# Four edits in the last two thirds of a graph-network kernel: chunk ends two products later, new PSUM places, spread stores, mixed rows inside a pass

## The chip, the core and the metric

The kernel runs on one NeuronCore of a Trainium2 chip. TensorE (PE) multiplies, VectorE (DVE) and ScalarE (ACT) work elementwise, GpSimd (POOL) and SyncE (SP) mostly start DMAs. Everything is float32. The metric is the device time of one execution in microseconds; the number compared is the median of the runs.

## The reference

N = 2708 nodes with 128 features, and a weighted sparse adjacency matrix `adj` (2708 x 2708) that is held dense. Four residual layers:

```python
x = layernorm(x + L0(x, adj))   # Laplacian product, 4 nearest neighbours, Laplacian product with them
x = layernorm(x + L1(x, adj))   # attention
x = layernorm(x + L2(x, adj))   # normalised Laplacian product
x = layernorm(x + L3(x, adj))   # relu([x, adj @ x] @ W.T + b)

# L1:
XW = X @ W
Z1 = leaky_relu((XW @ a[f:])[:, None] + (XW @ a[:f])[None, :], 0.01)
den = exp(Z1);  num = A @ den
att = where(num != 0, den / num, 0)
H = A @ (att @ XW)
```

## The kernel before

**Layout.** `adj` lies transposed in DRAM (`adjT`). A product with `adj` runs over 22 row tiles of 128 rows (the last, `FULL`, has 20 rows) and over six column chunks (four of 512 columns, one of 384, one of 276). `res` keeps the last six row tiles in SBUF, the others stream through the four slots of `ring`, one panel of four row tiles at a time, loaded by SP (L178). The 20 rows of the last tile are spread over three groups of partitions (`few`), so that the last-tile products of three chunks stand together.

**`by_panels` (L189)** is the pass that is run for the last three products with `adj`. For each chunk `c` it makes one product per row tile (L204; a float32 product is two matrix instructions) into a PSUM tile of the pool `acc`. In chunks 0 and 3 the last-tile products of three chunks follow (i == FULL). When a chunk is complete it calls `done(c, acc)`, which is `into_hT` (L231): ACT copies the chunk to `hT`/`gb` (L234), then `then(c, tiles)` runs: `end_layer1` transposes (L1794), `end_layer2` and `end_layer3` multiply by a weight (L285), and DVE, POOL and ACT do the norm. The passes are not in a hand-written order: the Tile scheduler places the instructions, so chunks 1, 2, 4 and 5 have the first product of the next chunk between their copy and what reads it; chunks 0 and 3 have nothing there.

**The attention loop (`block_layer`).** Ranking makes the matrix of L1 sparse enough for blocks: 44 steps (two column halves `h` of 22 steps `q`), in an order written out by hand for all engines. In step i, `load(i + 2)` fetches two gathers of rows by POOL (L1133) and, by SP, two short rows each from the table `carry` (L1140); POOL fetches rows of XW (L1113); PE finds `num` (L1699) for the narrow piece of step i and the wide piece of step i+1, then adds step i-1 into `hacc` (L1581); ACT inverts `num` with Ln and Exp (L1556, L1559); DVE corrects and weighs (L1566, L1570, L1573); SP stores two rows of each result back into `carry` (L1714). The narrow `num` has one PSUM buffer, the wide one two, `hacc` three banks. All of them come from one pool `ops`, so the wide buffers lie in banks 0 to 3, the narrow in bank 4, `hacc` in 5 to 7.

**The loop's head.** Before the loop, `add_line` (L1430) sums the whole matrix into two PSUM banks; `end_half(1)` copies the second to SBUF by ACT (L1450, L1451), SP sends it to `carry` in four DMAs (`send_half`, L1459) and loads last rows of `adjT` back into `res` (L1549), of which the scheduler leaves three on SP after the sends. Then every engine reads `flag` (L1592) and branches (L1851) into the arm that holds the loop. The first steps of the loop are the fill of a pipeline.

**Between the loop and the passes.** ACT and DVE copy `hacc` to `mT` (L160, L162), PE transposes twelve tiles of it (L1782), DVE scales them into `mixed`, which is the same place as `carry` (L1783). The first ten tiles were mixed already in the loop's last step (L1765, L1767). Then `by_panels(rows_of(mixed), ...)` begins. `acc2` (three banks) and `mis2` (five) are the pools of the passes.

## Time and profile before

| what | us |
|---|---|
| median of 3 runs | 1047.29 (1046.78 to 1047.69) |
| the profiled execution, its time | 1047.87 |
| its span, from first to last instruction | 1046.1 |
| PE busy | 980.2 (94%) |
| DVE, ACT, POOL busy | 638.9, 332.6, 263.4 |
| mean granted TensorE clock | 0.977 |
| up to the loop's head | 0 to 488 |
| attention loop | 488 to 711 |
| three passes | 711 to 1046 |

PE's busy time includes time in which one instruction drains while the next streams. Idle PE time is what matters where the chain of work runs through PE. In a row of the timeline, the bracket at the end gives how long the engine was idle before, and what the profile takes for the releaser. A row with a count merges instructions that follow each other, so gaps can lie within it. "issue" means that nothing in the profile shows the wait.

### The profile page before, as it was taken

Reading aid. Unit: us, or ns where it says so; the run is one execution under the profiler, and the core shown is the slowest. Engines: PE = TensorE matmul, PEld = TensorE weight load, DVE = VectorE, ACT = ScalarE, POOL = GpSimd, SP = SyncE. Lnnn points to the kernel's source line nnn. Section 1 sums busy time; section 2 is a strip of 40 time slices with the busy share of each in tenths; the row PEclk is TensorE's granted clock in tenths of the full one; section 3 lists DMA queues with packets and bytes.
Section 4 is the critical chain, followed back from the end, with each engine's and each line's share of the span. In section 5 each row is a group of like instructions: output and inputs, shape, how many; then the busy total and the mean of one; then the engine's idle time right before and its main releaser. Section 6 shows DMA issues by size and latency. Waiting matters only on the chain.

```text
span 1046.1 us, 11657 instructions
## 1 busy us (share of the span) xinstructions
PE 980.2 (94%) x3773; PEld 478.0 (46%) x3773; DVE 638.9 (61%) x1364; ACT 332.6 (32%) x609; POOL 263.4 (25%) x339
## 2 busy tenths in 40 slices
PE   0899999999987999798999999999999999999996
PEld 0346544444433456554333333334445544564444
DVE  5876549999834579864999999993212121222222
ACT  0000236555401235504677776661101100020000
POOL 5000000000665564027766444420111100000000
PEclk9899999999997999799999999999999999999998
DMA  9998220000383657696555455556564856474652
GB/s 344 351 366 259 91 81 1 1 0 1 94 276 93 220 166 239 232 414 190 156 170 148 137 147 158 142 178 235 168 229 150 308 187 223 141 262 164 215 174 71
DMA packets 100401, 187.85 MB, mean 180 GB/s; under 512 B 13958, under 2 KB 43278, under 8 KB 100330
## 3 DMA queue, kind: packets, MB, share of 16 engines
q1 hardware_dynamic: 82296, 149.19, 42.4%
q0 software_dynamic: 17728, 37.62, 12.5%
q8 instruction: 32, 0.52, 0.2%
q14 instruction: 39, 0.32, 0.1%
q10 hardware_dynamic: 306, 0.20, 0.1%
HBM read 211.66 MB, written 4.16 MB: 206 GB/s over the span
## 4 chain that ended last, share of the span: by engine, by line
PE 49%; DVE 1%; ACT 1%; issue 0%; DMA 0%; POOL 0%; POOLq 0%; DVEq 0%
PE acc L204 28%; PE hacc L1581 10%; PE num L1699 10%; PE mis L285 1%; PE mis L1828 0%; DVE inv L1570 0%; ACT gb L234 0%; DVE err L1566 0%; PE mis L1794 0%; DVE inv L1573 0%; PE mis L1824 0%; DMA ring<-carry 0%; POOL rstd L253 0%; PE mis L1782 0%; ACT m_rows L160 0%
## 5 line engine op out<-in xcount | busy, mean ns | idle before, releaser
L1133 POOL DMA_INDIRECT ring<-in_adjT,slot_i x88 | 94.4, 1073 | 95.5 <-PE num L1699 73.7
L1699 PE MATMUL num<-ring,lw 128*64 128x512 f32 (+1 forms) x528 | 112.4, 556 | 3.9 <-DVE err L1566 1.9
L1581 PE MATMUL hacc<-inv,xws 128*128 128x512 f32 (+1 forms) x264 | 111.7, 559 | 0.3 <-DVE inv L1573 0.3
L724 PE MATMUL acc<-zT,z 128*128 128x512 f32 (+2 forms) x252 | 102.2, 552 | 0.0
L1556 ACT ACTIVATE inv<-num,plain 128x1024 f32<-128x1024 f32 x88 | 80.6, 916 | 57.6 <-PE num L1699 40.1
L253 POOL TENSOR_TENSOR rstd<-rstd,minus_half 128x4 f32<-128x4 f32 (+1 forms) x18 | 17.3, 961 | 313.4 <-DVE rstd L252 313.4
L234 ACT COPY gb<-acc 128x512 f32<-128x512 f32 (+2 forms) x18 | 9.6, 536 | 251.0 <-PE acc L204 251.0
L725 ACT COPY key<-acc 128x512 f32<-128x512 f32 (+2 forms) x126 | 67.2, 536 | 54.9 <-PE acc L724 27.6
L204 PE MATMUL acc<-ring,y 128*128 128x512 f32 (+2 forms) x192 | 83.7, 566 | 0.5 <-issue 0.5
L769 POOL DMA_INDIRECT got<-y_rows,where x66 | 71.5, 1084 | 41.7 <-DVE near_sum L782 20.5
L1581 PEld LDWEIGHTS hacc<-inv,xws 128*128 128x128 f32 x264 | 46.5, 189 | 77.6 <-issue 53.2
L1566 DVE TENSOR_TENSOR err<-inv,num 128x1024 f32<-128x1024 f32 x88 | 74.7, 854 | 8.5 <-ACT inv L1559 7.3
L204 PE MATMUL acc<-ring,xs 128*128 128x512 f32 (+2 forms) x192 | 78.1, 550 | 0.0
L1573 DVE SCALAR_TENSOR_TENSOR inv<-gb,g_inv,inv 128x1024 f32<-128x1024 f32 x88 | 77.0, 914 | 0.1
L204 PE MATMUL acc<-ring,carry 128*128 128x512 f32 (+2 forms) x192 | 74.5, 542 | 0.0
L204 PE MATMUL acc<-ring,m_rows 128*128 128x512 f32 (+2 forms) x192 | 74.3, 542 | 0.0
L1570 DVE SCALAR_TENSOR_TENSOR inv<-err,inv 128x1024 f32<-128x1024 f32 x88 | 72.5, 862 | 0.1
L724 PEld LDWEIGHTS acc<-zT,z 128*128 128x128 f32 x252 | 45.8, 190 | 50.4 <-issue 45.0
L1559 ACT ACTIVATE inv<-inv 128x1024 f32<-128x1024 f32 x88 | 67.7, 769 | 2.8
L1699 PEld LDWEIGHTS num<-ring,lw 128*64 128x64 f32 x528 | 35.8, 137 | 62.3 <-issue 47.6
L728 DVE MAX8 near<-key 128x8 f32<-128x2708 f32 x21 | 62.3, 2966 | 2.7 <-ACT key L725 2.7
L593 POOL TENSOR_TENSOR slot_e<-near,sim 128x44 f32<-128x44 f32 (+2 forms) x3 | 0.7, 240 | 248.9 <-DVE near L590 248.8
(379 smaller groups left out, 1361.7 us busy)
## 6 DMA issues: line engine op xcount, KB each, us to landing
ring<-in_adjT SPq DMA_DIRECT2D x71, 1024.0 KB
ring<-in_adjT SPq DMA_DIRECT2D x20, 677.0 KB
ring<-in_adjT SPq DMA_DIRECT2D x17, 768.0 KB
part<-in_adjT SPq DMA_DIRECT2D x12, 1024.0 KB
ring<-in_adjT SPq DMA_DIRECT2D x17, 552.0 KB
more<-in_adjT SPq DMA_DIRECT2D x10, 677.0 KB
res<-in_adjT SPq DMA_DIRECT2D x4, 1280.0 KB
part<-in_adjT SPq DMA_DIRECT2D x3, 768.0 KB
```

The lines of the kernel that those rows point to most:

```text
L204: nc.tensor.matmul(accs[c][: lhsT.shape[-1], :w], lhsT=lhsT, rhs=src, start=start, stop=stop)
L724: nc.tensor.matmul(pks[c][:p, : cw[c]], lhsT=z2[:, :p], rhs=zT[:, cs], start=False, stop=True)
L725: nc.scalar.copy(key[:p, cs], pks[c][:p, : cw[c]])
L769: nc.gpsimd.indirect_dma_start(out=got[:p, :], out_offset=None, in_=y2_rows[:, :], in_offset=bass.IndirectOffsetOnAxis(ap=where[:p, t, k : ...
L1133: nc.gpsimd.indirect_dma_start(out=rows[i][:KC, n, :], out_offset=None, in_=adj_half[:, :], in_offset=bass.IndirectOffsetOnAxis(ap=slot_i[ ...
L1556: nc.scalar.activation(inv, num[:, :w], AF.Ln, scale=plain[:, 0:1], bias=plain[:, 1:2])
L1559: nc.scalar.activation(inv, inv, AF.Exp, scale=-1.0)
L1566: nc.vector.tensor_mul(err, inv, num[:, :w])
L1570: nc.vector.scalar_tensor_tensor(inv, err, 2.0, inv, op0=ALU.subtract, op1=ALU.mult)
L1573: nc.vector.scalar_tensor_tensor(inv, gb[:, col : col + w], g_inv[:, q : q + 1], inv, op0=ALU.max, op1=ALU.mult)
L1581: nc.tensor.matmul(haccs[:, o:e], lhsT=xws[:, q, :], rhs=inv[:, o:e], start=(q == 0), stop=(q == NQ - 1))
L1699: nc.tensor.matmul(num[n * (BJ + 2) : (n + 1) * (BJ + 2), o:e], lhsT=lw[:, 2 * q + n, :], rhs=rows[i][:, n, c0 + o : c0 + e], start=True, ...
```

## The change

1. In `by_panels`, `done` now only copies and returns the rest; for chunks 0 and 3 the rest is run when two further products have been issued. For the other chunks it is run at once, as before.
2. The copy of the second half of the heads is made by DVE instead of ACT. The loop's PSUM pool is split into four: `hacc` in banks 0 to 2, the narrow `num` in bank 3, odd wide ones in 4 and 5, even ones in 6 and 7. In the passes `mis2` comes first (banks 0 to 4), `acc2` after it (5 to 7).
3. The four sends of the second half and the loads of the last rows are taken from the loop's head and given to SP one at a time, in steps 4 to 7 and 8 to 13. Six loads of last rows are now in the arm, where before three of them had been placed earlier.
4. The first pass begins with eight products of row tiles mixed in the loop; then come the twelve transposes with two products between them.

In the built program the order on POOL is the same as before; on ACT only the copy is gone; on DVE only the copy is new and the mixing has another line; PE has the same instructions in the order that 1 and 4 say.

```diff
-    def by_panels(weights, done, tick=None, ready=(), first=None):
+    def by_panels(weights, done, tick=None, ready=(), first=None, between=(0, None)):
...
+        pending = Due()
         def product(c, i, src, w):
+            pending.tick()
...
-                    done(c, accs[c])
+                    rest = done(c, accs[c])
+                    if rest is not None:
+                        pending.at(pending.n + 3, rest)
...
                 product(c, i, src, w)
+                if c == 0 and i + 1 == between[0]:
+                    between[1]()
                 if i == FULL - 1 and c % GROUPS:
-                    done(c, accs[c])
+                    rest = done(c, accs[c])
+                    if rest is not None:
+                        rest()
...
             nc.scalar.copy(hT[:, cols[c]], acc[:, : cw[c]])
-            then(c, chunk_tiles[c])
+            return lambda: then(c, chunk_tiles[c])
...
-            nc.scalar.copy(tot[:, : edges[4] - edges[3]], banks[h][:, : edges[4] - edges[3]])
-            nc.scalar.copy(tot[:64, edges[4] - edges[3] :], banks[h][:64, edges[4] - edges[3] : span])
+            copy = nc.vector.tensor_copy if h else nc.scalar.copy
+            copy(tot[:, : edges[4] - edges[3]], banks[h][:, : edges[4] - edges[3]])
+            copy(tot[:64, edges[4] - edges[3] :], banks[h][:64, edges[4] - edges[3] : span])
...
-        send_half(1, heads[1], nc.sync)
-        for c in range(C):
-            nc.sync.dma_start(res[few(c), FULL - S, cols[c]], adjT[FULL * P :, cols[c]])
+        right = heads[1]
...
-            tc.tile_pool(name="ops", bufs=1, space=bass.MemoryType.PSUM) as ops,
+            tc.tile_pool(name="hops", bufs=1, space=bass.MemoryType.PSUM) as hops,
+            tc.tile_pool(name="nops", bufs=1, space=bass.MemoryType.PSUM) as nops,
+            tc.tile_pool(name="odd", bufs=1, space=bass.MemoryType.PSUM) as odd,
+            tc.tile_pool(name="even", bufs=1, space=bass.MemoryType.PSUM) as even,
...
+            def num_tile(n, w, name):
+                pool = nops if w == NARROW else (even, odd)[n % 2]
+                return pool.tile([P, w], F32, tag=f"num{w}", name=name)
...
+                    if 4 <= i < 8:
+                        send_half(1, right, nc.sync, (i - 4,))
+                    elif i - 8 in range(C):
+                        last_rows_back((i - 8,))
...
+        mis_pool = arm.enter_context(tc.tile_pool(name="mis2", bufs=5, space=bass.MemoryType.PSUM))
         acc_pool = arm.enter_context(tc.tile_pool(name="acc2", bufs=3, space=bass.MemoryType.PSUM))
-        mis_pool = arm.enter_context(tc.tile_pool(name="mis2", bufs=5, space=bass.MemoryType.PSUM))
...
-        by_panels(rows_of(mixed), into_hT(end_layer1))
+        by_panels(rows_of(mixed), into_hT(end_layer1), between=(first // 4 * 4, mix_rows))
```

`mix_rows` holds the loop over the twelve tiles (transpose, scale) that stood before the first pass, and `last_rows_back(chunks)` the loads of the last rows. `Due.at(n, f)` runs f at the n-th tick.

More of the change, by code (lines that the diff above doesn't have):

```diff
@@ L225, in by_panels @@
                 product(c, i, src, w)
+                if c == 0 and i + 1 == between[0]:
+                    between[1]()
                 if i == FULL - 1 and c % GROUPS:
-                    done(c, accs[c])
+                    rest = done(c, accs[c])
+                    if rest is not None:
+                        rest()
                 if tick is not None:
                     tick()
+        assert not pending.work
     def into_hT(then):
@@ L1449, in end_half, with send_half @@
             tot = heads[h]
-            nc.scalar.copy(tot[:, : edges[4] - edges[3]], banks[h][:, : edges[4] - edges[3]])
-            nc.scalar.copy(tot[:64, edges[4] - edges[3] :], banks[h][:64, edges[4] - edges[3] : span])
+            copy = nc.vector.tensor_copy if h else nc.scalar.copy
+            copy(tot[:, : edges[4] - edges[3]], banks[h][:, : edges[4] - edges[3]])
+            copy(tot[:64, edges[4] - edges[3] :], banks[h][:64, edges[4] - edges[3] : span])
             if h == 0:
                 send_half(h, tot, nc.scalar)
-        def send_half(h, tot, queue):
-            for g in range(4):
+        def send_half(h, tot, queue, groups=range(4)):
+            for g in groups:
                 w = edges[g + 1] - edges[g]
@@ L1592, with last_rows_back @@
     over = nc.values_load(flag[0:1, 0:1], min_val=0, max_val=N)
+    def last_rows_back(chunks):
+        for c in chunks:
+            nc.sync.dma_start(res[few(c), FULL - S, cols[c]], adjT[FULL * P :, cols[c]])
     def dense_layer():
@@ L1606, in dense_layer @@
             nc.sync.dma_start(y2g[:LAST, FULL, :], y2_rows[FULL * P :, :])
+            last_rows_back(range(C))
             load_x(range(T))
@@ L1690, in block_layer @@
             nums, invs, haccs = {}, {}, {}
-            pieces = {"wide": (0, WIDE, 2), "narrow": (WIDE, NARROW, 1)}
+            pieces = {"wide": (0, WIDE), "narrow": (WIDE, NARROW)}
+            def num_tile(n, w, name):
+                pool = nops if w == NARROW else (even, odd)[n % 2]
+                return pool.tile([P, w], F32, tag=f"num{w}", name=name)
             def find_num(i, piece):
-                q, (c0, w, bufs) = steps[i][1], pieces[piece]
-                num = nums[i, piece] = ops.tile([P, w], F32, tag=f"num{w}", name="num", bufs=bufs)
+                q, (c0, w) = steps[i][1], pieces[piece]
+                num = nums[i, piece] = num_tile(i, w, "num")
                 for o in range(0, w, CW):
@@ L1707, in keep @@
             def keep(i, piece, err):
-                (h, q), (c0, w, _) = steps[i], pieces[piece]
+                (h, q), (c0, w) = steps[i], pieces[piece]
                 for n in range(2):
@@ L1720, in add @@
                 if q == 0:
-                    haccs[h] = ops.tile([P, 3 * CW], F32, tag="hacc", name="hacc")
-                for piece, (c0, w, _) in pieces.items():
+                    haccs[h] = hops.tile([P, 3 * CW], F32, tag="hacc", name="hacc")
+                for piece, (c0, w) in pieces.items():
                     add_up(w, q, invs[i, piece], haccs[h][:, c0 : c0 + w])
@@ L1748, in block_layer @@
                         errs = {}
-                        for piece, (c0, w, _) in pieces.items():
+                        for piece, (c0, w) in pieces.items():
                             errs[piece] = mix_1(w, nums[i, piece], invs[i, piece], own)
@@ L1753, in block_layer @@
                             mix_2(invs[i, piece], errs[piece])
-                        for piece, (c0, w, _) in pieces.items():
+                        for piece, (c0, w) in pieces.items():
                             mix_3(w, q, invs[i, piece], h * HALF + c0)
                     else:
-                        for piece, (c0, w, _) in pieces.items():
+                        for piece, (c0, w) in pieces.items():
                             mix_2(invs[i, piece], mix_1(w, nums[i, piece], invs[i, piece], own))
                             mix_3(w, q, invs[i, piece], h * HALF + c0)
-                for t0 in range(0, EARLY, WIDE // P):
+                for n, t0 in enumerate(range(0, EARLY, WIDE // P)):
                     ts = range(t0, min(t0 + WIDE // P, EARLY))
-                    pt = ops.tile([P, WIDE], F32, tag=f"num{WIDE}", name="pt", bufs=2)
+                    pt = num_tile(len(steps) + n, WIDE, "pt")
                     for t in ts:
@@ L1774, in two_layers, with mix_rows @@
         nonlocal acc_pool, mis_pool, hT
+        mis_pool = arm.enter_context(tc.tile_pool(name="mis2", bufs=5, space=bass.MemoryType.PSUM))
         acc_pool = arm.enter_context(tc.tile_pool(name="acc2", bufs=3, space=bass.MemoryType.PSUM))
-        mis_pool = arm.enter_context(tc.tile_pool(name="mis2", bufs=5, space=bass.MemoryType.PSUM))
         hT = gb
-        for t in range(first, T):
-            p = pw[t]
-            pt = mis_tile()
-            nc.tensor.transpose(pt[:p, :D], mT[:, t * P : t * P + p], ident)
-            nc.vector.tensor_scalar_mul(mixed[:p, t, :], pt[:p, :D], f_out[:p, t : t + 1])
-        spread(mixed[:, FULL, :])
+        def mix_rows():
+            for t in range(first, T):
+                p = pw[t]
+                pt = mis_tile()
+                nc.tensor.transpose(pt[:p, :D], mT[:, t * P : t * P + p], ident)
+                nc.vector.tensor_scalar_mul(mixed[:p, t, :], pt[:p, :D], f_out[:p, t : t + 1])
+            spread(mixed[:, FULL, :])
         inv_sqrt_of(dinv, deg, DEG_EPS)
+        if not first:
+            mix_rows()
         y3 = m_rows
```

## The prediction

> **What bounds the kernel now.** I read the page first, then the chain of work that ended last, then the timeline at its breaks.
>
> ```profile
> PE 980.2 (94%) x3773; PEld 478.0 (46%) x3773; DVE 638.9 (61%) x1364; ACT 332.6 (32%) x609; POOL 263.4 (25%) x339
> ```
>
> PE is the bound, so in its span of 1046.1 us the change can only win where PE stands idle or slow on the path: at the head of the attention loop, between loop and first pass, and at chunk ends. The chain through the head, and the timeline of PE there:
>
> ```profile
> 494.35 2.07 DMA ring<-carry
> ...
> 500.79 2.47 PE hacc L1581 x6
> 503.26 2.42 PE num L1699 x12
> ```
>
> ```profile
> 488.31 4.30 PE L1699 MATMUL num<-ring,lw 128*64 128x512 f32 x20 [0.74 <-issue]
> 494.50 0.78 PE L1699 MATMUL num<-ring,lw 128*64 128x330 f32 x4 [1.88 <-DVE err L1566]
> 496.55 4.24 PE L1699 MATMUL num<-ring,lw 128*64 128x512 f32 x8 [1.28 <-DMA ring<-carry]
> ```
>
> Three waits (the third ends 0.13 after the short load's landing): 0.74, 1.88 and 1.28 us. The eight instructions of the third row take 4.24 us. From 500.79 on, a step is 2.47 + 2.42 = 4.89 us and PE never waits until the loop's end. What stood before these rows on SP and ACT, and on DVE beside them:
>
> ```profile
> 488.06 0.15 ACT L1451 COPY m_rows<-acc 64x1 f32<-64x1 f32 x1
> 488.24 3.63 SPq L1459 DMA_DIRECT2D carry<-m_rows  x4
> 491.91 1.26 SPq L1549 DMA_DIRECT2D res<-in_adjT  x3
> 494.35 1.42 SPq L1140 DMA_DIRECT2D ring<-carry  x2
> 495.90 1.75 DVE L1573 SCALAR_TENSOR_TENSOR inv<-gb,g_inv,inv 128x1024 f32<-128x1024 f32 x2
> ```
>
> SP gave out seven DMAs, the flag and the branch before step 2's two short loads. And the clock granted around the third wait (columns: stretch, length, busy time of PE, PEld, DVE, ACT, POOL, then PEclk, DMA share, GB/s):
>
> ```profile
> 493.00:496.50 3.50, 0.78 (x4) 0.20 (x4) 3.50 (x5) 3.44 (x6) 2.99 (x3) 1.00 0.43 108
> 496.50:500.70 4.20, 4.15 (x8) 1.17 (x8) 4.20 (x7) 0.72 (x2) 3.28 (x4) 0.59 0.59 152
> ```
>
> Last, the chain from the loop's end into pass 1 and over the first chunk's end:
>
> ```profile
> 708.51 2.55 PE hacc L1581 x6
> ...
> 712.92 0.76 PE mis L1782 x5
> 713.69 0.86 PE acc L204 x2
> ...
> 716.17 17.46 PE acc L204 x44
> 733.63 0.59 ACT gb L234
> ```
>
> PE stands from 711.06 to 712.92 for three copies one after another, and again at 733.63 for one copy. A product (two instructions) is 0.86 us here.
>
> **The change part by part.**
>
> *Head, start of PE.* In the built program the first `num` waited for ACT's copy L1451, whose PSUM bank it reuses; that copy ended at 488.21 and PE's weight load began at 488.28. In the changed program it waits only for the loads of step 0, and the narrow and the odd piece for readers that ended by 486.3. What is left between the last matrix instruction (487.57) and the first one is flag and branch. No PE row shows their cost, so I bound it: nothing gives a gain of 0.74, all of it gives 0. DVE went through the same pair in 0.45 (487.41 after 486.96), ACT in 0.15; that is 0.29 and 0.59. I take 0.45, between these two nearest rows. DVE gets the copy (two instructions, 0.59 on ACT); it had nothing to do until 492.81 except one 0.18 us row for `dinv`, which then ends near 489, before POOL comes to its power at 489.58. Hidden; if it were late, POOL's gathers of step 3 would be. ACT's table load (1.28) moves ahead of 488 as well, but it ended at 489.64 before, under PE's first piece: nothing.
>
> *Head, third wait.* The two loads of step 2 now stand directly behind flag and branch on SP. SP is free of the loads of steps 0 and 1 at 481.4, and their own waits are ring lines that PE finished near 484.5. At 2.07 us from issue to landing they are there by 488, seven us early. The gathers of step 2 were issued at 484.18 and 487.15 and end their issue at 488.21; with the same 2.07 after that and their own transfer they land near 491. So wide piece 2 runs when narrow piece 1 ends, 495.28, for 8 x 4.30 / 20 = 1.72: until 497.0, instead of 500.7. Narrow piece 1 itself still waits for DVE's row of step 0 (one buffer), so the 1.88 stays. Next is `hacc` of step 0. It needs DVE's L1573, whose wide part ends at 497.18 and narrow part at 497.65. So `hacc` begins at 497.24 instead of 500.72: **3.48** us. From there PE repeats in 4.89 and DVE in 4.75 (495.90 to 500.66 in these rows), so DVE does not catch PE up. Step 3's gathers (issued until 496.52, DMA activity falls off near 499.5) and its short loads (behind the stores of step 0, issued by 497.9, landing near 499.9) meet a need at about 500: a margin near zero, which I price at 0 to 0.5 of loss and take as 0.1.
>
> The 3.48 includes the low clock of 496.5 to 500.7. Does it come back? [...] At 711.0 to 713.0 a gap of 1.87 let the clock stay at 1.00. I take full clock; half clock for 3.4 us would cost 1.7 and leave 1.8 of the 3.48.
>
> *SP inside the loop.* Ten steps get one more DMA.
>
> ```profile
> 537.14 1.23 SPq L1140 DMA_DIRECT2D ring<-carry  x2
> 539.47 2.47 SPq L1714 DMA_DIRECT2D carry<-err  x4
> ```
>
> The added DMA stands behind the two short loads and ahead of the next four stores. There SP is idle from 538.37 to 539.47, 1.10 us. A send costs 3.63 / 4 = 0.91 and a load of last rows 1.26 / 3 = 0.42: both fit, so nothing is delayed. If the cover were gone, the stores would slip and the loads behind them too; these land at 540.4, PE needs them at 542.9, so 2.4 us more are spare. The loads land in `res` some 170 us before pass 1 reads them.
>
> *Between loop and pass 1.* The eight products read tiles that ACT mixed by 710.75; `acc2` now lies in banks 5 to 7, whose last reader is that same ACT row, not in those that are being copied. The first panel was issued at 694.93, the second at 699.81, the others at 704.70, and the DMA stops at about 711.5. So PE goes from the last `hacc` straight on, and the copies (711.09 to 712.87) lie under 6.9 us of products. After these the order of before repeats: five transposes, product, five, product, two, and DVE's 0.28 per tile keeps its pace. Gone is 711.06 to 712.92, plus the drain and refill at the break, 0.0 to 0.27: I take **2.0**.
>
> *Chunk ends.* Chunk 0 of pass 1 costs from 733.63 to 734.92, 1.29. Where a product lies between, as at chunk 1, four transposes cost 0.47. So 0.82. Alike chunk 3 of pass 1 (791.04 to 792.34), chunks 0 and 3 of pass 2 (835.44 to 837.22, 894.34 to 896.14, against 0.98), chunk 3 of pass 3 (1010.00 to 1011.79): 0.83, 0.80, 0.82, 0.81, **4.1** in all. Two products are 1.7 us (1.3 in the narrower chunk 4) over a copy of 0.59. Chunk 0 of pass 3 brings nothing: its copy at 947.29 already lies under other last-tile products, and L285 follows at 950.03 with no wait for ACT. PSUM tiles and panels are there; norms start 1.7 us later and have 15 us of slack.
>
> That chunk has the other fall of the clock, 0.50 from 951 to 954, after a stretch in which PE is recorded busy all the time, but with 20-row products and small ones. It costs about 1.7. The change puts two full products into that stretch. [...] Bounds: 0 to 1.7 gain. I take 0, since the stretch ahead of the two products is as it was.
>
> Sum: 0.45 + 3.48 - 0.1 + 2.0 + 4.1 = **9.9**. The profiled span goes from 1046.1 to 1036.2, its time (1.8 more) from 1047.87 to 1038.0. The median of the runs is 0.6 below that execution: 1047.29 - 9.9 = **1037.4**.
>
> **The rivals.**
> (a) Half clock returns in the head, or falls at a new place (an idle gap of 1.88 stays there): +1.7, 1039.1. For: 0.59 in the row above. [...]
> (b) The fall at 951 does not come: 1035.7. [...] Against: it starts right after an unchanged stretch.
> (c) The third wait was not the short load: the gathers or DVE bind in its place, and of the head only 0.5 to 1 us is won: 1040.5. Against: PE restarts just after the landing.
> (d) Slower: the added DMAs hold SP up. An issue waits for the DMA eight before it on its queue. If it took over 1.1 + 2.4 = 3.5 us instead of 0.91, in ten steps, each us beyond that is paid on PE. From 4.5 us each it takes all of the 9.9 back; at 5 us, 1052. For: SP's queue is 76% full in a step. Against: every row of it there is 0.6 to 0.9 per DMA.
> That the change does nothing is excluded at the chunk ends by the order of the built program.
>
> **How the numbers follow.** My forecast 0.56, (a) 0.13, (b) 0.19, (c) 0.08, (d) 0.04. The first alone has 1036.4 to 1038.4 (start of PE 0 to 0.74, drains, step 3). With (a) and (b) and half a us around each: 1035.0 to 1039.7, leaving out (c), (d) and tails. 0.2% is 2.1 us, about what can be told from no change; (a) to (c) are all beyond it. Faster 0.94, within 0.2% 0.02, slower 0.04.
>
> **What would show it.** PE's first `num` within 0.5 us of the last `add_line`; no wait for ring<-carry; first `hacc` near 496.8; clock 1.00 in the head; a step of 4.89 also in steps 4 to 13; no PE gap at the loop's end; no wait of L1794 or L285 for ACT in chunks 0 and 3. The prediction is wrong if steps with an added DMA are longer, or if half clock shows in new places.

## The result

| | kernel before | changed kernel |
|---|---|---|
| median, on the same chips | 1048.14 (22 runs) | 1045.03 (22 runs) |
| ratio | | 0.9952, 95% interval 0.9936 to 0.9968 |
| profiled execution: its time, its span | 1047.87, 1046.1 | 1042.87, 1041.0 |
| forecast | | 1037.4 (1035.0 to 1039.7) |

Times are in us. By the ratio the change makes the kernel faster by 0.48%, which is 5.0 us of 1048 (3.4 to 6.7 by its interval); the two medians themselves stand 3.1 apart, and the two profiled spans 5.1. The runs of each kernel scatter over 10 to 12 us. Forecast were 9.9, so the direction was right and about half of the gain is missing; the time lies outside the range that was given.

The first row of the page of the changed kernel shows PE as full as before:

```profile
PE 981.2 (94%) x3773; PEld 478.1 (46%) x3773; DVE 638.7 (61%) x1366; ACT 331.8 (32%) x607; POOL 272.7 (26%) x339
```

The timeline of PE at the loop's head, changed kernel (start, length, instruction, idle time before it and its releaser):

```profile
486.10 1.34 PE L1439 MATMUL acc<-res,lc 128*32 128x339 f32 x16
487.38 4.22 PE L1721 MATMUL num<-ring,lw 128*64 128x512 f32 x20
493.45 2.50 PE L1721 MATMUL num<-ring,lw 128*64 128x330 f32 x12 [1.86 <-DVE err L1574]
496.29 2.51 PE L1589 MATMUL hacc<-inv,xws 128*128 128x512 f32 x6 [0.34 <-ACT inv L1567]
498.73 1.63 PE L1721 MATMUL num<-ring,lw 128*64 128x330 f32 x6
500.76 1.91 PE L1721 MATMUL num<-ring,lw 128*64 128x512 f32 x6 [0.40 <-issue]
502.59 2.54 PE L1589 MATMUL hacc<-inv,xws 128*128 128x512 f32 x6
505.06 3.31 PE L1721 MATMUL num<-ring,lw 128*64 128x330 f32 x12
508.30 1.98 PE L1589 MATMUL hacc<-inv,xws 128*128 128x512 f32 x4
```

The first and the third wait of before are gone, and the first `hacc` sum starts at 496.29 instead of 500.72. (Step 1 is counted from the start of the first `hacc` sum to the start of the second, and so on.) But steps 1 and 2 are 6.30 and 5.71 long instead of 4.89: the twelve `num` instructions, 2.42 of work, are broken by an idle gap at 500.36 and take 3.31 at 505.06. The same happens twice more, in steps 7 and 8 (PE's timeline there):

```profile
530.35 2.80 PE L1721 MATMUL num<-ring,lw 128*64 128x330 f32 x12
...
535.55 3.34 PE L1721 MATMUL num<-ring,lw 128*64 128x330 f32 x12
```

What these instructions wait for is shown by PE's weight loads, which stand ahead of them (steps 1, 2 and 8):

```profile
500.73 0.23 PEld L1721 LDWEIGHTS num<-ring,lw 128*64 128x64 f32 x4 [1.25 <-DMA ring<-in_adjT,slot_i]
506.44 0.23 PEld L1721 LDWEIGHTS num<-ring,lw 128*64 128x64 f32 x4 [0.63 <-DMA ring<-in_adjT,slot_i]
536.96 0.20 PEld L1721 LDWEIGHTS num<-ring,lw 128*64 128x64 f32 x4 [0.66 <-DMA ring<-in_adjT,slot_i]
```

`ring<-in_adjT,slot_i` is the gather by POOL, each time the second one of its step.

The passes came out as forecast. The chain of the changed kernel goes from the last sum straight into products, and at the first chunk's end from product to transposes without ACT's copy:

```profile
707.45 2.54 PE hacc L1589 x6
709.99 6.89 PE acc L206 x16
716.88 0.55 PE mis L1810 x5
717.42 0.86 PE acc L206 x2
...
719.91 12.42 PE acc L206 x32
732.33 0.44 PE mis L1823 x4
732.77 2.58 PE acc L206 x6
```

In the last pass, half clock lasts twice as long as before. Changed kernel, the stretch of half clock (columns as in the earlier table by stretch):

```profile
943.00:950.00 7.00, 7.00 (x15) 3.44 (x15) 1.15 (x5) 0.00 (x0) 0.00 (x0) 0.51 0.00 0
```

The account of the two profiles, changed minus before, in us:

| place | forecast | measured |
|---|---|---|
| everything ahead of the loop's head | 0 | -0.13 |
| last `add_line` to first `num` | -0.45 | -0.80 |
| first `num` to first `hacc` sum (12.41, now 8.91) | -3.48 | -3.50 |
| steps 1 and 2 | +0.1 | +2.22 |
| steps 7 and 8 | 0 | +1.15 |
| loop's end to pass 1 | -2.0 | -1.9 |
| five chunk ends | -4.1 | -3.9 |
| half clock in pass 3 (3.41, now 6.83 long) | 0 | +1.7 |
| sum | -9.9 | -5.2 |

So of the 4.7 that are missing, 3.3 lie in the loop's steps and 1.7 in the half clock; the start of PE gave some back.

Two questions were open: what takes 3.4 us in the loop, and whether the longer half clock belongs to the change.

### The profile page after: what moved, and what is told of

It is laid out like the page before. It is cut to its first block, busy times and chain, and to the rows that moved or that the text cites. A ratio compares the mean times of both kernels' runs of the same rounds, so it can differ in the third digit from the quotient of the medians.

```text
span 1041.0 us, 11657 instructions
## 1 busy us (share of the span) xinstructions
PE 981.2 (94%) x3773; PEld 478.1 (46%) x3773; DVE 638.7 (61%) x1366; ACT 331.8 (32%) x607; POOL 272.7 (26%) x339
## 4 chain that ended last, share of the span: by engine, by line
PE 89%; DVE 5%; issue 2%; ACT 2%; DMA 1%; POOL 0%; SPq 0%; POOLq 0%; DVEq 0%; ACTq 0%
PE acc L206 37%; PE num L1721 10%; PE hacc L1589 10%; PE acc L733 10%; PE acc L437 9%; PE acc L1439 3%; PE acc L723 3%; DVE both L516 2%; DMA res<-in_adjT 1%; PE mis L294 1%; ACT junk L961 1%; PE mis L1164 1%; PE mis L828 1%; PE sl L1280 1%; PE mis L533 1%
## 5 line engine op out<-in xcount | busy, mean ns | idle before, releaser
L1142 POOL DMA_INDIRECT ring<-in_adjT,slot_i x88 | 105.6, 1200 | 85.6 <-PE num L1721 59.3
L1581 DVE SCALAR_TENSOR_TENSOR inv<-gb,g_inv,inv 128x1024 f32<-128x1024 f32 x88 | 77.1, 915 | 0.1
L1578 DVE SCALAR_TENSOR_TENSOR inv<-err,inv 128x1024 f32<-128x1024 f32 x88 | 72.3, 860 | 0.1
L1567 ACT ACTIVATE inv<-inv 128x1024 f32<-128x1024 f32 x88 | 67.6, 768 | 2.8
```

The source lines that it names most:

```text
L1142: nc.gpsimd.indirect_dma_start(out=rows[i][:KC, n, :], out_offset=None, in_=adj_half[:, :], in_offset=bass.IndirectOffsetOnAxis(ap=slot_i[ ...
L1567: nc.scalar.activation(inv, inv, AF.Exp, scale=-1.0)
L1578: nc.vector.scalar_tensor_tensor(inv, err, 2.0, inv, op0=ALU.subtract, op1=ALU.mult)
L1581: nc.vector.scalar_tensor_tensor(inv, gb[:, col : col + w], g_inv[:, q : q + 1], inv, op0=ALU.max, op1=ALU.mult)
```

## The experiments

For each run the table gives the ratio to the kernel before, measured beside it, then from one profiled execution: the time from the first `num` to the first `hacc` sum, what steps are longer than 4.89 and by how much, how long half clock lasted between first `num` and step 3 and in pass 3, and the passes' length (end of the last `hacc` sum to the end). "Loss" below is the sum of the longer steps.

| kernel | ratio (95%) | first sum | longer steps | half clock: head, pass 3 | passes |
|---|---|---|---|---|---|
| before | 1 | 12.41 | none | 3.4, 3.4 | 335.0 |
| changed | 0.9952 (0.9936 to 0.9968) | 8.91 | 1: 1.41, 2: 0.81, 7: 0.30, 8: 0.85 | 0, 6.8 | 331.0 |
| after_again | 0.9945 (0.9921 to 0.9970) | 8.91 | 1: 1.01, 2: 1.40, 7: 0.60, 8: 0.95 | 0, 0 | 327.6 |
| passes_only | 0.9955 (0.9935 to 0.9974) | 10.79 | 1: 1.20 | 0, 3.4 | 329.1 |
| head_only | 0.9970 (0.9949 to 0.9991) | 8.91 | 1: 1.15, 2: 1.31, 14: 1.46 | 0, 6.8 | 335.0 |
| sends_late | 0.9943 (0.9922 to 0.9964) | 8.91 | 1: 1.22, 2: 1.06, 6: 0.23, 7: 1.73 | 0, 0 | 327.8 |
| fetch_late | 0.9919 (0.9893 to 0.9946) | 8.91 | 1: 1.73, 6: 1.40 | 0, 3.4 | 329.3 |
| lead_dummy | 0.9974 (0.9953 to 0.9996) | 10.88 | 2: 1.20, 4: 1.62, 7: 1.04, 8: 0.42 | 0, 3.4 | 329.4 |
| dinv_late | 0.9936 (0.9914 to 0.9958) | 9.01 | 1: 0.92, 25: 1.04 | 0, 3.4 | 329.4 |
| dinv_early_again | 0.9906 (0.9870 to 0.9942) | 9.39 | 1: 0.49, 7: 1.04, 8: 0.14 | 0, 3.4 | 329.3 |
| early_sends | 0.9914 (0.9886 to 0.9942) | 9.47 | 1: 0.46, 7: 1.15 | 0, 3.4 | 329.5 |
| early_all | 0.9917 (0.9888 to 0.9946) | 9.01 | 7: 1.41, 8: 0.39 | 0, 0 | 327.6 |
| all_four | 0.9931 (0.9904 to 0.9958) | 9.00 | 7: 0.25, 12: 2.19, 13: 1.70, 28: 0.14 | 0, 6.8 | 331.4 |
| *measured where before takes 1034 to 1035* | | | | | |
| after_third | 0.9921 (0.9901 to 0.9941) | 8.91 | 1: 0.38, 2: 0.44, 8: 0.08 | 0, 3.4 | 329.5 |
| dinv_twice | 0.9947 (0.9929 to 0.9964) | 8.91 | 1: 3.52, 6: 0.18, 7: 0.34 | 0, 3.4 | 329.5 |
| before_early | 0.9993 (0.9978 to 1.0008) | 12.94 | 1: 0.17 | 6.8, 0 | 333.6 |
| dinv_early | 0.9929 (0.9912 to 0.9946) | 9.96 | 1: 0.28 | 3.4, 3.4 | 329.2 |
| early_shorts | 0.9922 (0.9905 to 0.9939) | 9.97 | 1: 0.28 | 3.4, 3.4 | 329.2 |
| shorts_every | 0.9919 (0.9898 to 0.9939) | 10.10 | 1: 0.14 | 3.4, 6.8 | 331.2 |
| shorts_sends | 0.9920 (0.9899 to 0.9942) | 9.88 | 1: 0.36 | 3.4, 3.4 | 329.4 |

The lower block was measured where the kernel before takes 1034 to 1035; in the measurements of the upper block it takes 1048 to 1051. The record gives the number of a chip, and number 9 stands in both blocks (dinv_early's group below, lead_dummy's above), so it is open whether the chips differ or something else did. Comparisons below stay within a block unless they say otherwise.

### One half of the change at a time

**passes_only** has edits 1 and 4 on the kernel before:

```diff
-            copy = nc.vector.tensor_copy if h else nc.scalar.copy
+            copy = nc.scalar.copy
...
-        right = heads[1]
+        send_half(1, heads[1], nc.sync)
+        for c in range(C):
+            nc.sync.dma_start(res[few(c), FULL - S, cols[c]], adjT[FULL * P :, cols[c]])
```

(The sends and loads in the loop's steps go, and the PSUM pools are in the order of before.)

> The kernel before with edits 1 and 4 alone (chunk ends, products ahead of the mixing); PSUM places, copy by ACT, sends and loads of last rows as before. By the two traces these edits brought 1.9 us at the loop's end and 3.9 at five chunk ends. Theory of separate stages: the loop's head as before (first sum of hacc 4.1 to 4.4 us later than in the changed kernel against the last add_line), every step of the loop 4.89, and 5.7 us less than before if pass 3 has the same length of half clock. Rival, that the passes win less when the loop ends later (panels or clock): under 4.5 us with the same half clock.

**head_only** has edits 2 and 3 alone:

```diff
-                        pending.at(pending.n + 3, rest)
+                        rest()
...
-        if not first:
-            mix_rows()
+        mix_rows()
...
-        by_panels(rows_of(mixed), into_hT(end_layer1), between=(first // 4 * 4, mix_rows))
+        by_panels(rows_of(mixed), into_hT(end_layer1))
```

> The changed kernel with edits 1 and 4 undone; the head (PSUM places, copy by DVE, spread sends and loads) stays. Theory: the head wins 4.3 us at the first sum of hacc and gives 2.2 back in steps 1 and 2 and 1.15 in steps 7 and 8, so the loop ends 1 us earlier than before against its own start, and the kernel gains about 1 us. Rival, that the stalls in steps 1, 2, 7 and 8 were chance of one execution: loop end 4 us earlier, gain 4 us.

Measured were 4.7 us (by the ratio, of 1049.97) for the passes and 3.1 for head_only. The intervals of the two ratios overlap, and only the profiles separate the parts. With 3.4 of half clock in pass 3 the passes take 335.0 in the old order (before) and 329.1 to 329.5 in the new one (six profiles of the upper block): 5.5 to 5.9, against 6.1 forecast. At full clock it is 333.6 (before_early, of the lower block) against 327.6 to 327.8. So the passes are right.

head_only, in which edit 4 is undone, has no gap at the loop's end either (PE's timeline):

```profile
707.40 2.54 PE L1589 MATMUL hacc<-inv,xws 128*128 128x512 f32 x6 [0.27 <-DVE inv L1581]
709.78 2.75 PE L206 MATMUL acc<-ring,carry 128*128 128x512 f32 x6
712.37 0.71 PE L1810 MATMUL mis<-ident,m_rows 128*128 128x128 f32 x5
```

Here the scheduler itself puts three products ahead of the transposes, and 2.6 us are enough to cover copies of 1.8. The new PSUM places of the passes' pools are the likely reason; no run has them alone. The 2.0 of the loop's end can be had without edit 4, and with the 1 us expected of the head it makes up nearly all of head_only's 3.1.

passes_only has the old head, and there half clock happened to stay away (PE's timeline):

```profile
501.02 2.87 PE L1722 MATMUL num<-ring,lw 128*64 128x512 f32 x8 [1.04 <-DMA ring<-carry]
...
506.28 1.63 PE L1722 MATMUL num<-ring,lw 128*64 128x330 f32 x6
508.07 1.90 PE L1722 MATMUL num<-ring,lw 128*64 128x512 f32 x6 [0.16 <-DMA ring<-carry]
```

The first sum comes 10.79 after the first `num`, 1.62 sooner than in the profile of before, and step 1 is then 1.20 longer. So of what the slow clock cost the old head, 1.2 of 1.6 was no real cost: the rows of step 3 were not there any sooner.

### POOL's power

POOL's timeline in the changed kernel shows what stands ahead of the gathers of step 3 (493.76 and 495.81):

```profile
487.01 1.28 POOL L1142 DMA_INDIRECT ring<-in_adjT,slot_i  x1 [2.49 <-issue]
488.59 1.03 POOL L1122 DMA_INDIRECT xws<-xw_rows,row_j  x1 [0.30 <-DVE dinv L261]
489.65 3.90 POOL L262 TENSOR_TENSOR dinv<-dinv,minus_half 128x22 f32<-128x22 f32 x1
493.76 1.74 POOL L1142 DMA_INDIRECT ring<-in_adjT,slot_i  x1 [0.20 <-issue]
495.81 1.27 POOL L1142 DMA_INDIRECT ring<-in_adjT,slot_i  x1 [0.30 <-issue]
497.38 1.03 POOL L1122 DMA_INDIRECT xws<-xw_rows,row_j  x1 [0.30 <-issue]
498.72 1.90 POOL L1142 DMA_INDIRECT ring<-in_adjT,slot_i  x1 [0.30 <-issue]
500.93 1.37 POOL L1142 DMA_INDIRECT ring<-in_adjT,slot_i  x1 [0.30 <-issue]
```

The second gather of step 3 leaves POOL at 497.08, its last landing record stands at 500.26, and PE goes on at 500.76. The second short load of step 3 was late as well: issued at 496.60, it has its last record at 500.13. So two things arrive at nearly the same time, and taking away one of them cannot free PE. POOL is busy back to back from 488.59 on. Theory A: the power (3.90) for `dinv`, which nobody reads before pass 1, is the source of the lost steps. The rivals: B, the gathers are slow in their transfer; C, for steps 7 and 8, the DMAs added to SP.

**dinv_late** puts the power into step 24:

```diff
-        inv_sqrt_of(dinv, deg, DEG_EPS)
...
+                    if i == 24:
+                        inv_sqrt_of(dinv, deg, DEG_EPS)
                     find_num(i, "narrow")
```

> The changed kernel; the power that makes dinv (POOL, 3.9 us, in the head) and its addition (DVE) are moved to step 24 of the loop. Theory A: the power holds up POOL's gathers for step 3, and POOL, with no slack in a step, never catches up until its fetches of XW end: without it steps 1 and 2 take 4.9 each and 7 and 8 too, the loop ends 3.2 us earlier, the kernel gains about 3 us over the changed one. Rival B: the gathers are late by their own transfer (two under way at a time, 4 to 5.5 us from issue to landing): steps 1 and 2 still lose over 1.5 us, no gain over 0.7. Rival C, for steps 7 and 8: the added DMAs of SP cause these losses: steps 1 and 2 are cured, 7 and 8 still lose 1.1.

**sends_late** moves the DMAs that edit 3 spread:

```diff
-                    if 4 <= i < 8:
-                        send_half(1, right, nc.sync, (i - 4,))
-                    elif i - 8 in range(C):
-                        last_rows_back((i - 8,))
+                    if 16 <= i < 20:
+                        send_half(1, right, nc.sync, (i - 16,))
+                    elif i - 24 in range(C):
+                        last_rows_back((i - 24,))
```

> The changed kernel; the four sends stand in steps 16 to 19 and the six loads of last rows in steps 24 to 29, where POOL fetches nothing more. If the added DMAs cause the 1.15 us lost in steps 7 and 8, these steps now take 4.9 and the loop ends 1.15 earlier. If POOL's lag alone causes it, steps 7 and 8 lose about the same again. Steps 1 and 2 lose 2.2 either way, and steps 16 to 29 stay at 4.9.

With the power away, step 2 loses nothing and step 1 still 0.92; the power costs 1.04 in step 25 instead, since it meets the gathers there too. B, which had 1.5 or more lost in these two steps, falls. With the sends away nothing gets better: 4.2 are lost, of them 1.96 in steps 6 and 7. C falls.

**dinv_early** puts the power where POOL is idle, in the ranking, and **before_early** does the same to the kernel before. **dinv_twice** has a second power behind the first:

```diff
+            inv_sqrt_of(dinv, deg, DEG_EPS, power=True)
             nc.vector.scalar_tensor_tensor(f_out, deg, 0.0, f_r, op0=ALU.is_gt, op1=ALU.mult)
...
-        inv_sqrt_of(dinv, deg, DEG_EPS)
```

```diff
         inv_sqrt_of(dinv, deg, DEG_EPS)
+        twin = const.tile([P, T], F32, tag="twin", name="twin")
+        inv_sqrt_of(twin, deg, DEG_EPS)
```

> The changed kernel, with the power for dinv (3.90 us on POOL) and its add on DVE moved out of the loop's head to the ranking, where POOL stood idle for 16.46 us. What is compared is the stretch from the last add_line to the end of the last hacc sum: 223.93 us in the profile of before, 222.99 in that of the changed kernel. Theory A (the steps lost behind the head are POOL's lateness, and the power is its source): steps 2, 7 and 8 lose nothing, step 1 loses at most the 0.9 that it lost with the power in step 24; the stretch takes 220.6, the median lies 2.4 below that of the changed kernel. Theory B (the gathers are slow by their transfer or by the added DMAs of steps 4 to 13): steps 7 and 8 or others near still lose about 1.1 in sum, the stretch stays at 222 to 223, and the median within 1 us of the changed kernel's.

> The changed kernel with a second power of the same size (to a tile that nobody reads) behind the first on POOL. Theory A: POOL has next to no time to spare in the first 8 steps (fetch and two gathers fill the step's 4.9), so all or nearly all of the 3.90 us comes back on PE: the stretch from the last add_line to the end of the last hacc sum takes 226 to 227, the median lies 3 to 4 above that of the changed kernel. Theory B: POOL catches up from step to step, and the stretch grows by less than 1 us.

> The kernel before with the power for dinv moved as in dinv_early. Theory A: in the kernel before the first hacc sum is 3.5 to 4.4 us later, held by the short loads, and POOL's gathers come in time behind it unless the low clock is absent; so the move gains 0 to 1.2 us, the stretch takes 222.3 to 223.9. Rival: the power costs the kernel before as much as the changed one, 2.4 us: the stretch takes 221.5, and the head's edit would then be worth as much as was forecast.

In dinv_early no step after the first is longer, as A says; but half clock fell into the head there and delayed the first sum by 1.05, which helps. dinv_twice loses 4.0 in all. Its step 1 waits twice for gathers (PE's timeline):

```profile
489.41 1.07 PE L1721 MATMUL num<-ring,lw 128*64 128x512 f32 x2 [1.15 <-DMA ring<-in_adjT,slot_i]
491.60 1.93 PE L1721 MATMUL num<-ring,lw 128*64 128x512 f32 x6 [1.12 <-DMA ring<-in_adjT,slot_i]
```

In the same block the changed kernel itself (after_third, below) loses 0.9, so a second power of 3.9 us on POOL cost 3.1 there: A's dose, nearly. (Against the 3.4 and 4.0 lost by the changed kernel in the upper block it would have seemed to cost next to nothing.) before_early gains nothing (0.9993): the old head waits for its short load longer than for POOL.

**after_again** is the changed kernel once more, with **dinv_early_again** beside it. **fetch_late** leaves the power and takes three fetches from POOL (first diff below). **early_all** moves the power to the ranking, takes the three fetches away too and gives out the short loads of step 3 ahead of the stores of step 0 (second diff; `load` then leaves them out). **early_shorts** is dinv_early with these short loads alone:

```diff
-                    if late_q:
+                    if late_q and i >= 3:
                         fetch_xw(xws, late_q.pop(0))
```

```diff
+                        if i == 0:
+                            rows[3] = strip(3).rearrange("p (n k) -> p n k", n=2)
+                            for n in range(2):
+                                load_short(3, n)
                         for piece, (c0, w) in pieces.items():
                             errs[piece] = mix_1(w, nums[i, piece], invs[i, piece], own)
                             keep(i, piece, errs[piece])
```

> As dinv_early, and the two short loads of step 3 are given to SP ahead of the four stores of step 0 instead of behind them. Theory A with the short loads as the rest of step 1's loss: step 1 takes 4.9 too, the stretch from the last add_line to the end of the last hacc sum takes 219.7, and the median lies about 3.3 below that of the changed kernel. Rival: what is left of step 1's loss is the second gather of step 3; then the stretch stays at 220.6 as in dinv_early.

> The changed kernel once more, for a second profile of its loop and as the base of the other three on this chip. If the steps lost are a property of the kernel and not of one execution, 2 to 4.3 us are lost again between the first hacc sum and step 14 (3.38 in the first profile), and the stretch from the last add_line to the end of the last hacc sum takes 222.5 to 224. If they were chance, it takes 219.6. Ratio to before 0.995.

> The changed kernel with the power left in the head, but POOL is relieved in another way: the loop's fetches of XW rows begin in step 3 instead of step 0, which takes three instructions of 1.03 and their 0.30 gaps, 4 us, from POOL between the power and step 3. Theory A (POOL's lateness): POOL catches up before step 3; steps 2, 7 and 8 lose nothing, step 1 loses 1.0 or less, the stretch takes 220 to 221, the median lies 2 to 3 below that of the changed kernel. Rival: the losses follow from the power's presence in some way that has nothing to do with POOL's queue; then the stretch stays at 223.

> The power in the ranking, as in dinv_early, once more beside the changed kernel on one chip. Theory A: the median lies 2.0 to 3.5 below that of the changed kernel; no step after step 2 is longer than 4.9; where the head runs at full clock the stretch takes 219.6 to 220.5 and step 1 loses up to 0.9 (the short loads of step 3), where half clock falls into the head it takes 221.

> The power in the ranking, the fetches from step 3 on, and the short loads of step 3 ahead of the stores of step 0. If the short loads hold step 1 when POOL is in time, step 1 takes 4.9 here at full clock too, and the stretch takes 219.5; if not, step 1 loses 0.9 as before and the stretch takes 220.4. At half clock in the head 221 either way. The median is 2.5 to 4 below that of the changed kernel.

The losses of the changed kernel are its own: 3.96 in the second profile, in the same four steps. In dinv_early_again POOL waits for PE instead of running behind it (its timeline; compare 493.76 above):

```profile
489.29 1.04 POOL L1142 DMA_INDIRECT ring<-in_adjT,slot_i  x1 [0.67 <-PE num L1722]
490.64 1.05 POOL L1142 DMA_INDIRECT ring<-in_adjT,slot_i  x1 [0.31 <-issue]
```

Over the upper block: with the power in the head and the fetches in place, steps 1 and 2 lose 2.2 to 2.5 in sum (changed, after_again, head_only, sends_late). Where POOL is relieved, by either means, step 2 loses nothing in six of six. So POOL's queue, with the power in it, is shown to be the source of step 2's loss. Of step 1's it is hardly any: from the first `num` to the end of step 1 it is 14.8 to 15.2 with the power in the head and 14.8 without (dinv_late, dinv_early_again, early_sends), since the short loads of step 3 are then what comes last. In dinv_late the gathers have landed at 496.96 and 498.19, the two short loads at 502.54 and 503.22, and PE's products follow each short load by 0.13. fetch_late shows the same on PE:

```profile
506.35 1.90 PE L1721 MATMUL num<-ring,lw 128*64 128x512 f32 x6 [0.72 <-DMA ring<-carry]
```

With POOL relieved and these loads given out earlier step 1 takes 4.9 and ends 13.9 after the first `num` (early_all, all_four). early_shorts, which was to move them alone, could not tell, since half clock had covered that wait.

The power alone does not clear steps 7 and 8: in dinv_early_again they still lose 1.18, in early_all 1.80, with POOL in time. The chains of work that ended last name what came last in step 7, in this order for sends_late, dinv_early_again, early_all and early_sends:

```profile
525.96 7.39 DMA ring<-in_adjT,slot_i
523.92 5.62 DMA ring<-carry
524.05 5.47 DMA ring<-carry
530.41 5.76 DMA ring<-carry
```

With the power in the head (sends_late, and the changed kernel's row at 536.96 above) it is a gather, 7.39 from the start of its issue to landing; where POOL is in time it is a short load, 5.5 to 5.8 after its issue. In before the short loads of these steps took up to 5.0, and nothing was lost. So it is the same pair as in step 1: behind the late gathers stand late short loads.

### Steps 6 to 14

**lead_dummy** adds 2.47 of products ahead of the first sum, to test whether the loop only takes back a lead that it needs:

```diff
+                    if i == 1:
+                        haccs[0] = hops.tile([P, 3 * CW], F32, tag="hacc", name="hacc")
+                        for o in range(0, HALF, CW):
+                            e = min(HALF, o + CW)
+                            nc.tensor.matmul(
+                                haccs[0][:, o:e], lhsT=xws[:, 0, :], rhs=rows[1][:, 0, o:e], start=True, stop=True
+                            )
                     if i:
                         add(i - 1)
```

**early_sends** is dinv_early with the DMAs of sends_late, **all_four** is early_all with them.

> The changed kernel with one more set of three products (six instructions, 2.47 us, written into the banks of hacc and overwritten by the first sum) ahead of the first hacc sum. 0.34 of it falls into a wait, so the first sum starts 2.1 us later, 11.0 after the first num instead of 8.9. Theory 1 (the loop needs a lead, and takes it from PE in whichever step): the later steps lose 2.1 less than the 3.4 and 4.0 of the two profiles of the changed kernel, 1.2 to 2.0 in sum, and the stretch from the last add_line to the end of the last hacc sum stays at 222.7 to 223.9; the median is within 1 us of the changed kernel's. Theories 2 and 3 (losses of their own size in steps 2 to 14): the stretch takes 225 to 226, the median lies 2 above that of the changed kernel.

> The power in the ranking, and the sends in steps 16 to 19 and loads of last rows in steps 24 to 29: POOL and SP are both relieved in the first 14 steps. Theory 3: steps 2 to 14 lose nothing, the stretch takes 220.3 to 220.6 with up to 0.9 lost in step 1. Theory 1: 1.0 to 1.8 are lost in steps 6 to 14 as in dinv_early_again and early_all, unless half clock has already delayed the head by 1 us; the stretch takes 221 to 222.

> The power in the ranking, the fetches from step 3 on, the short loads of step 3 ahead of the stores of step 0, and the sends and last rows in steps 16 to 29: all that was added or stood in the way of the first 14 steps is out of them. Theory 1: early_all's 1.8 in steps 7 and 8 remain or come in a neighbouring step, the stretch takes 221.0 to 221.8. Theory 3: no step is longer than 4.9, the stretch takes 219.5.

lead_dummy's later steps lose 4.3, not 1.2 to 2.0, and its ratio is 2.2 to 2.9 per mille above the changed kernel's: theory 1 falls, although step 1 alone behaves as it says (its loss is gone). early_sends still loses 1.15 in step 7: added DMAs on SP are not the cause either. all_four has lost even more, 4.3, mostly in steps 12 and 13. The 1.70 of its step 13 is half clock: 3.41 us of it follow at 565.51 on the stall of step 12. In three long stalls PE waits for ACT, not for a DMA: lead_dummy's step 4, all_four's step 12, head_only's step 14 (fetch_late's step 6, with ACT idle for 4.09, looks the same). ACT's and PE's timeline in lead_dummy:

```profile
520.96 1.20 ACT L1564 ACTIVATE inv<-num,plain 128x1024 f32<-128x1024 f32 x1 [4.32 <-PE num L1721]
...
523.59 2.54 PE L1589 MATMUL hacc<-inv,xws 128*128 128x512 f32 x6 [1.55 <-ACT xws L1777]
```

ACT itself had stood idle for 4.32, by the profile for PE. Why, no row shows.

**shorts_every** gives out every step's short loads ahead of the stores, three steps ahead; **shorts_sends** moves the added DMAs too; **after_third** is the changed kernel beside them:

```diff
+                        if i + 3 < len(steps):
+                            rows[i + 3] = strip(i + 3).rearrange("p (n k) -> p n k", n=2)
+                            for n in range(2):
+                                load_short(i + 3, n)
```

> The power in the ranking; in every step SP gives out the two short loads of step i+3 ahead of the four stores of step i instead of behind them, about 2.5 us earlier, and the stores 1.3 us later. If the short loads are what steps 1 and 6 to 8 wait for: no step is longer than 4.9, the stretch from the last add_line to the end of the last hacc sum takes 219.5 at full clock in the head, the median lies 3 to 4 below that of the changed kernel. If the gathers land late too (rows of steps 9 and 10), 1.0 to 1.8 stay in steps 6 to 8 and the stretch takes 220.5 to 221.5.

> As shorts_every, with the sends in steps 16 to 19 and the loads of last rows in steps 24 to 29. If the DMAs added to SP delay its queue in steps 4 to 13 beyond what shorts_every cures: no loss here where shorts_every still has one, the stretch 219.5. If SP has no part in it: the same loss in both.

> The changed kernel as the base on this chip. 3 to 4.3 us lost in steps 1 to 14, the stretch 222.5 to 224, the ratio to before 0.995.

They can't tell it, since here the changed kernel itself loses next to nothing there: 0.08 in steps 3 to 14, 0.90 in all. It gains 8.2 us by the ratio (the medians are 1026.26 and 1034.76), near the forecast; in the upper block it was 5.0 and 5.8 (after_again), and the intervals overlap.

The four kernels of this block that have the power moved are no faster (0.9919 to 0.9929, against 0.9921), but they were not compared on equal terms: all four met 3.4 us of half clock in the head, the two with the power in the head met none.

What differs in this block is seen ahead of the loop. The stretch from 300 to 440 us (length, busy times, granted clock, DMA share, GB/s), first of before in the upper block, then of after_third:

```profile
300.00:440.00 140.00, 122.85 (x663) 72.65 (x666) 90.73 (x323) 49.12 (x97) 71.80 (x69) 0.90 0.60 195
```

```profile
300.00:440.00 140.00, 129.49 (x785) 77.21 (x783) 102.13 (x354) 50.35 (x103) 71.79 (x70) 0.93 0.67 222
```

222 instead of 195 GB/s. The loop's head is reached 12 us sooner, and POOL reaches its power sooner within it, 1.2 us after the first `num` instead of 2.3:

```profile
476.23 3.88 POOL L262 TENSOR_TENSOR dinv<-dinv,minus_half 128x22 f32<-128x22 f32 x1 [0.23 <-DVE dinv L261]
480.33 1.10 POOL L1142 DMA_INDIRECT ring<-in_adjT,slot_i  x1 [0.22 <-issue]
```

That fits A for steps 1 and 2, whose loss is 0.82 here. For steps 6 to 14 of the upper block, which lose 1.2 to 4.1 us in ten of eleven profiles with the new head (dinv_late is the exception), two things stay open: why the short loads of these steps take 5.5 us and more, and why ACT stalls. Taken away without making the sum smaller were: the power, the fetches of three steps, the short loads of step 3, the added DMAs. Not tried there: short loads ahead of the stores in every step, which is what the waits of step 7 ask for. One more thing lies near: between 520 and 545 us the trace of the changed kernel has four transfers of instruction code (8 or 16 KB); but before has four there as well and loses nothing.

### With the power moved: perhaps faster

Measured side by side in the upper block, the median of dinv_early_again is 1039.64 (6 runs), of the changed kernel 1044.12, of before 1051.48; but the intervals of the two ratios overlap (0.9870 to 0.9942, 0.9921 to 0.9970), so the gain over the changed kernel is not shown by the times. By the profiles the stretch from the start of the last `add_line` to the loop's end takes 221.5 to 221.8 in dinv_late, dinv_early_again, early_sends and early_all, 222.7 to 223.9 in the kernels with the power in the head, lead_dummy (225.8) aside; all_four, with its stall in step 12 and the half clock after it, took 224.0 in spite of the power's move. By this stretch the move of the power is worth 1 to 2 us where POOL is late.

## Why the prediction was half right

**Start of PE**, 0.45 taken: 0.80. The upper bound of 0.74 was the truth, and the first `num` even starts 0.07 before the modelled end of the last `add_line`: flag and branch cost PE nothing that shows, so the values from DVE's and ACT's rows (0.29, 0.59) were too careful.

**Third wait**, 3.48: 3.50. The short load was the wait, and its removal brings what was worked out. The next wait came as forecast: DVE's wide L1581 ends at 496.14, 0.15 ahead of the first sum (the profile names ACT's L1567, which ends at 496.21).

**Step 3's gathers and short loads**, "a margin near zero, which I price at 0 to 0.5 of loss and take as 0.1": this is the step that failed. It cost 2.22 in steps 1 and 2. The queue was the right one ("if it were late, POOL's gathers of step 3 would be"), but the sum was made with old times. Need was put at about 500, the old 503.5 less the 3.48 of the third wait; the earlier start of PE was not taken off, and need came at 499.1. The second gather was given the old 499.5 to land. In before it landed at 499.25, too late for 499.1 even so; now its issue ended 0.57 later and it landed at 500.26, since the two gathers took POOL 1.74 and 1.27 instead of 1.10 and 1.43. The second short load was given 2.07 to land and took 3.5 or more. And only step 3 was looked at: step 4's gathers stand behind those of step 3 with no gap on POOL, so that step 2 lost another 0.81.

**"From there PE repeats in 4.89"** (nothing lost in steps 4 to 13, the added DMAs at 0): steps 7 and 8 lost 1.15. The added DMAs did cost nothing that shows: SP gave out a send in 0.80 and a load of last rows in 0.41, and moving them did not help. DVE and SP had been held against the step of 4.89; POOL had not. Between 517 and 533 a fetch and two gathers (1.03, 1.64, 1.31) with three gaps of 0.30 fill 4.88 of it, so POOL cannot catch up, and step 8 waits for its second gather. With POOL relieved the short loads come next; why they are slow there is open.

**Half clock in the head**: it did not come in the three profiles of the changed kernel, so the choice of full clock was right. PE was busy for 2.71 of the 3.50 us from 493.0 to 496.5 in the first of them, against 0.78 in before, but no run isolates what decides (see the last section). Its price, 3.4 us at a cost of 1.7, follows from the 0.59 over 4.20 us in before; measured were 3.41 and about 1.75. But the gain counted for full clock was not right: passes_only shows 1.2 of it as cover for step 3's rows.

**Half clock in pass 3**, 0: +1.7 in the profile, by chance. The passes of the same code ran with 0, 3.4 or 6.8 us of it (after_again, passes_only, changed), and took 327.6, 329.1 and 331.0. It says nothing on the change. That the stretch ahead of it was unchanged, given as the reason for 0 and against rival (b), was no argument.

**Loop's end**, 2.0: 1.9. **Chunk ends**, 4.1: 3.9. Right, by the same steps, save that the loop's end did not need edit 4.

Of the faster rivals, (c) with 1040.5 came nearest to the 1045.0 of the changed kernel, but for another reason: the third wait was the short load, and the gathers became the next.

## What to carry to other kernels

When a wait in the fill of a pipeline is removed, everything that feeds the next steps is needed sooner by the same amount: go through each queue for as many steps as it prefetches, with the issue times that the new order gives, not those of the old trace, and hold what each queue does in a step against the step's length. Look there for work that nobody needs yet, such as a power of 3.9 us ahead of gathers, and move it to where its engine idles. When a late transfer is cured and the step stays long, look for a second one that lands just behind it. A half-clock stretch in one profile is to be checked in a second profile before it is put down to a change.

## What was not expected of the hardware

- Half clock lasted 3.41 or 6.83 us, no other length, wherever it was measured in the head and in pass 3 in these kernels (ahead of the loop also 13.65, in before and in the changed kernel; the last one, from 1039.54 in before and 1035.32 in the changed kernel, still lasts at the end and is not counted here). The same code met it in one execution and not in another: in pass 3 the changed kernel had 6.83 us of it, after_third 3.4 and after_again none. In the new order the passes took 327.6 to 327.8 without it, 329.1 to 329.5 with 3.4 us and 331.0 to 331.4 with 6.8, so each 3.4 us costs about 1.75. What decides no run isolates. In the head of before PE was busy for 1.03 of the 3.41 us ahead of it (493.40 to 496.81). Two stretches nearer to each other, in dinv_early and in after_third, each with the one that follows:

```profile
477.89:481.31 3.42, 1.46 (x10) 0.48 (x8) 2.67 (x3) 3.36 (x5) 2.17 (x3) 1.00 0.64 177
481.31:484.72 3.41, 3.41 (x9) 0.99 (x6) 3.41 (x6) 2.11 (x5) 2.72 (x2) 0.50 0.47 136
```

```profile
478.97:482.38 3.41, 1.55 (x10) 0.63 (x10) 2.97 (x4) 3.35 (x5) 2.89 (x3) 1.00 0.16 23
482.38:485.80 3.42, 3.08 (x11) 1.09 (x8) 3.42 (x6) 3.36 (x6) 2.81 (x3) 1.00 0.69 203
```

  In the first stretch PE pauses for 1.96 us, in the other for 1.86. Ahead of the half clock in pass 3 PE was recorded busy throughout (3.42 of 3.42 us from 939.74 to 943.16 in the changed kernel), but in part with products of 20 rows.
- The same gather took POOL 1.04 to 1.94 us to issue in the changed kernel. Between 517 and 533 a fetch and two gathers fill the step there (above); in before they took 1.21, 1.05 and 1.05. The eleven of 1.62 or more up to 560 us began while DVE's L1578 ran (those at 493.76 and 498.72 beside rows of 1.63 at 493.32 and 498.07), but one of 1.04 at 543.37 lies beside such a row too (543.73). What makes them longer no run isolates.
- The same program took 14 us less in some measurements than in others (1034 against 1048 to 1051), with one number of a chip on both sides. What makes the difference is open; a ratio is only good against runs of before made beside it.
